# Window attention in float32: scores of two heads per matmul and a product over 128 rows of keys, with zeros where heads or windows differ, and bands fetched at other times

## The chip, the cores and the metric

The kernel runs on one core of one Trainium2 chip. The metric is the device time of one execution in microseconds (us); the kernel before was timed three times, and its time is the median of the three. One further execution was taken with the hardware profiler; its page and trace are what this document reads. TensorE is called PE in the profile (its weight loads PEld), VectorE is DVE, ScalarE ACT, GpSimd POOL and SyncE SP.

## The reference, cut to what matters

The input `x` has 16 images of 56 x 56 pixels with 384 channels, float32.

```python
x = x + attention(groupnorm(x))       # layer 0
x = x + depthwise3x3(groupnorm(x))    # layer 1, weights clipped and taken as signs

def attention(x):                     # shifted windows of 7 x 7
    x = roll(x, (-3, -3), axis=(1, 2))
    q, k, v = split(x @ w_qkv.T, 3)   # 12 heads of 32 channels
    # per image: 64 windows of 49 tokens, 12 heads
    score = q @ k.T / sqrt(32) + relative_position_bias   # 49 x 49 a window and head
    score = where(mask of the last window row / column, -inf, score)
    out = softmax(score) @ v
    return roll(out @ w_out.T + b_out, (3, 3), axis=(1, 2))
```

## The kernel before, in words

**Tiling.** Channels lie on partitions: 384 channels are `NC` = 3 blocks of 128 (four heads of 32 in a block, `HPC`), tokens run along the free dimension. A *strip* `s` is one row of eight windows (8 x 49 = 392 tokens, `ST`); an image has `NS` = 8 strips, the batch 128. A strip is worked in two *units* of four windows (`UW`), so there are 256 units, 16 for each image; below, the first unit of a strip is called even and the second odd.

**One unit** (`heavy` and `all_units`). TensorE's work stands in a list of six slots, written out by hand, and every engine works through its instructions in the program's order. In the even unit the slots are three blocks `value` (v of the next strip, L485) and three blocks `query_key` (q of the next strip, L472); in the odd unit three blocks `query_key` (k of the next strip) and three blocks `project` (L656, this strip's output). Each block is 3 float32 matmuls of 392 columns into one of four rotating PSUM banks; ScalarE copies q, k (L479) and v (L492) out, DVE adds the projected block to `x` (L664). After slot 0 come, for the unit's own windows, `add_up` (L597: a matmul with ones that sums the exponentials over keys), `invert` (L635 logarithm and L636 exponential on ScalarE, then L637 and L638 on DVE), `attend` (L617: attention weights times v; ScalarE copies the result to `ot` at L627) and `divide` (L645 on DVE). The next unit's `scores` (L526) and `softmax` (L543, DVE: scale and bias from PSUM to the tile `es`) come after slot 2 in the even unit (before q is overwritten) and after slot 3 in the odd one; its `exponential` (L561, ScalarE) one slot later. `normalize` (L461) makes the input of the strip after next, in slot 4 of the odd unit.

**Scores and product before.** `scores` makes, per unit, 4 windows x 12 heads = 48 matmuls: 32 channels of one head on the rows, 64 key columns as weights, 49 query columns streamed. Keys come out on partitions: window `w` = 0 of a pair on rows 0 to 48, window 1 on rows 64 to 112, so `es` holds two windows side by side on the partitions. `attend` therefore makes 48 matmuls too: 49 keys of one window on the rows (the lower or the upper half of the array), 32 value channels of one head as weights, 49 columns.

**v by keys.** `turn` (L496, DVE) transposes v in 32 x 32 blocks and `by_key` (L508) moves it with 16 DMAs per strip on SP's queue, in slots 3 and 5 of the even unit, to the tile `vs`, with keys on partitions.

**Light work.** The depthwise layer of the image before, and the loads of the next image, are spread over the units by due times (`at(when, ...)`, in units; a list sorted by time is emptied between slots). `plan_conv` places, for each of six chunks of an image (2 halves x 3 channel blocks, one every `step` = 2.6 units): `band` (L703, SP's queue: 28 rows and their neighbours from DRAM into the one buffer of `bpool`), `pad` (L748, ScalarE, 1624 elements) and `middle` (L778, ScalarE, 1568 elements), both of which read the band, eight `tap` (L784, DVE), `turn_sum` (L791) and eight `store` (L798, SP's queue). `plan_load` places the gathers of the next image's rows: DMAs on POOL's queue (L419), a transpose on DVE (L436) and `arrange` (L448 and L451, ScalarE).

**End.** `plan_last` does the last image's depthwise layer after the last unit, partly on TensorE (`convolve`, L822; `carry`), partly as taps on DVE.

Of the kernel before, what the change touches and what calls it, by code (L numbers as in the profile page):

```python
# [19 lines left out]
NEG = -1.0e30  # L20
# [14 lines left out]
def kernel(  # L35
# [65 lines left out]
    least = const.tile([P, 1], F32, tag="least", name="least")  # L101
    reach = const.tile([P, 2, B * NU], F32, tag="reach", name="reach")
    seen = const.tile([P, B + NC], F32, tag="seen", name="seen")
# [15 lines left out]

    es = const.tile([P, NH, 2, HT], F32, tag="e", name="e")  # L120

# [16 lines left out]
    def clear_more():  # L138
        nc.gpsimd.memset(power, -0.5)
        nc.gpsimd.memset(ones, 1.0)  # L140
        nc.gpsimd.memset(least, LEAST)
        nc.gpsimd.memset(seen, 0.0)
        for t in (qk[:, :, ST:], *hps, *accs):
            nc.gpsimd.memset(t, 0.0)

    def clear_again():
        for t in (qk[:, :, ST:], *spare):
            nc.vector.memset(t, 0.0)
# [41 lines left out]
    def load_bias(queue, first_q, last_q, fast):  # L190


        if not loaded_bias:
            rel = ypool.tile([P, NC, WIN, R], F32, tag="y", name="rel").rearrange("q c h w -> q (c h w)")[:, : T * NH]
            nc.gpsimd.memset(rel, 0.0)
            loaded_bias.append(rel)
        rel = loaded_bias[0]
        flat = rel.rearrange("q (a n) -> q a n", a=WIN)
        for q in range(first_q, last_q):
            qr, qc = divmod(q, WIN)  # L200
            first = qr * REL + qc if fast else (WIN - 1 - qr) * REL + (WIN - 1 - qc)
# [12 lines left out]
        nc.gpsimd.memset(mask, 0.0)  # L214
        for w in range(2):
            queue.dma_start(mask[w * HT : w * HT + T], wmask[0:T, :, 0:T])
        loaded_bias.append(mask)

    def add_bias(fast):
# [5 lines left out]
        for v in range(2):  # L225
            for w in range(2):
                for i in range(HPC):
                    nc.vector.tensor_tensor(
                        bias[:, v, i * NC : (i + 1) * NC, w, :],
                        rel_n[:, i],  # L230
                        mask[:, v].unsqueeze(1).to_broadcast([P, NC, T]),
                        ALU.add,
                    )

# [234 lines left out]
    def query_key(s, m):  # L469
        pq = bank(f"pq_{s}_{m}")  # L470
        for c in range(NC):
# [6 lines left out]
            )  # L478
        nc.scalar.copy(qk[:, m, :ST], pq[:, :ST])  # L479

# [32 lines left out]
    def scores(u, fast):  # L513
# [4 lines left out]
        for j in range(NC):  # L518
            for w in range(2):
                for r in range(2):  # L520
                    for i in range(HPC):
                        part = slice(i * D, (i + 1) * D)
                        q0 = (n * UW + 2 * r + w) * T
                        row, col = (w, r) if fast else (r, w)
                        k0 = (2 * j + col) * T
                        nc.tensor.matmul(  # L526
                            pp[row * HT : (row + 1) * HT, i, k0 : k0 + T],
                            qk[part, NC * fast + j, q0 : q0 + HT],
                            qk[part, NC * (not fast) + j, q0 : q0 + T],
                            start=True,  # L530
                            stop=True,
                        )
        raw[u] = pp

    def softmax(u, fast):

        s = u // UPS
        pp = raw[u]
        e = es.rearrange("k (i j) w q -> k i (j w) q", i=HPC)[:, :, :, :T]
        if fast:  # L540
            flat = es.rearrange("k h w q -> k (h w q)")[:, : NH * 2 * T]
            e = flat.rearrange("k (i n q) -> k i n q", i=HPC, q=T)
        nc.vector.scalar_tensor_tensor(  # L543
            e,
            pp[:, :, : NC * 2 * T].rearrange("q i (n k) -> q i n k", k=T),
            QSCALE,
            bias[:, int(s % NS == NS - 1)].rearrange("q (i j) w k -> q i (j w) k", i=HPC),
            ALU.mult,
            ALU.add,
        )  # L550
        if fast:
# [6 lines left out]
    def exponential(u, fast):  # L558
        if fast:
            flat = es.rearrange("k h w q -> k (h w q)")[:, : NH * 2 * T]  # L560
            nc.scalar.activation(flat, flat, AF.Exp, accum_out=reach[:, 0, u : u + 1])  # L561
            return
# [20 lines left out]

    def by_head(u):

        flat = es.rearrange("k h w q -> k (h w q)")[:, : NH * 2 * T]
        return flat.rearrange("k (h r q) -> k h r q", h=NH, r=2)

    def add_up(u):

        e = by_head(u)
        su = raw[u][:, :, NC * 2 * T : NC * 3 * T]
        for r in range(2):
            for i in range(HPC):
                for w in range(2):
# [3 lines left out]
                        ones[keys, :D],  # L599
                        e[keys, i * NC : (i + 1) * NC, r],  # L600
                        start=True,
# [4 lines left out]
    def attend(u, fast):  # L606
        s, n = divmod(u, UPS)
        if n == 0:
            ots[s] = two.tile([P, NC, ST], F32, tag="ot", name=f"ot_{s}")
        po = [bank(f"po_{u}_{w}") for w in range(2)]  # L610
        for j in range(NC):
            for r in range(2):
                for i in range(HPC):
                    for w in range(2):
                        h = HPC * j + i
                        keys = slice(w * HT, w * HT + T)
                        nc.tensor.matmul(  # L617
                            po[w][i * D : (i + 1) * D, (2 * j + r) * T : (2 * j + r + 1) * T],
                            vs[s][keys, n * 2 + r, h * D : (h + 1) * D],
                            by_head(u)[keys, i * NC + j, r] if fast else pts[u, j][keys, 2 * i + r, :],  # L620
                            start=True,
                            stop=True,
                        )
        ot = ots[s][:, :, n * UW * T : (n + 1) * UW * T]
        by_window = ot.rearrange("p j (r w q) -> p j r w q", r=2, w=2)
        for w in range(2):
            nc.scalar.copy(  # L627
                by_window[:, :, :, w, :], po[w][:, : NC * 2 * T].rearrange("p (j r q) -> p j r q", j=NC, r=2)
            )

# [77 lines left out]
    def band_late(b, k, c, part):  # L708
# [4 lines left out]
        if part == 0:  # L713
# [3 lines left out]
            elif (k, c) == (0, 1):  # L717
                xb = qk.rearrange("p m n -> p (m n)")
            elif (k, c) == (1, 0):
                xb = bias.rearrange("p v h w n -> p (v h w n)")  # L720
            else:
# [82 lines left out]

    def convolve(b, k, c):

# [4 lines left out]
        tiles = LR * W // OT  # L811
        summed[k] = []
        for first in range(0, tiles, 4):
            n = min(4, tiles - first)
            pc = bank(f"pc_{k}_{first}")
            summed[k].append((first, n, pc))
            for i in range(n):
# [13 lines left out]
    def carry(b, k, c):  # L831

        by_token = spare[k].rearrange("p t c -> p (t c)")
        tiles = LR * W // OT
# [30 lines left out]
    def plan_last(b, first):  # L865
# [8 lines left out]
        for n, (k, c) in enumerate(chunks):  # L874
# [27 lines left out]
    def plan_conv(p, first, step, lead, late, queue):  # L902
# [116 lines left out]
    with tc.manual_schedule():  # L1019
# [29 lines left out]
        worst = small.tile([P, 2], F32, tag="worst", name="worst")  # L1049
        for n in range(2):  # L1050
            nc.vector.tensor_scalar(reach[:, n], reach[:, n], MOST[n], None, ALU.is_lt)
        nc.vector.tensor_reduce(worst[:, 0:1], reach.rearrange("p n u -> p (n u)"), AX.X, ALU.min)
# [73 lines left out]
```

## Time and profile before

| | us |
|---|---|
| three timed runs | 4202.64, 4207.44, 4210.01 |
| median | 4207.44 |
| the profiled execution, its whole time | 4213.37 |
| the same, from first to last instruction (span) | 4211.4 |

| engine | busy us | share of the span |
|---|---|---|
| TensorE matmuls | 4068.7 | 97% |
| TensorE weight loads | 2565.1 | 61% |
| DVE | 3495.2 | 83% |
| ScalarE | 2232.3 | 53% |
| POOL | 1863.9 | 44% |

The granted TensorE clock was 0.988 of full speed over the span. How to read the lines: a row of groups has line, engine, operation, output tile <- input tiles, shape, count, then busy time in us and mean ns of one, then the idle time of that engine just before it and what ended most of it. A float32 matmul stands as two records, each with its own weight load. A row of waits has who waited, for whom, total us, how many times, longest. A row of the timeline has start and duration in us, engine, line, operation, and in square brackets the idle time before it with its releaser. Matmul ends are modelled and overlap, so a block of matmuls is best measured from its start to the next block's start.

### The profile page before, as it was taken

The page shows a single profiled execution, that of the slowest core. Times are in us where ns is not written, and L with a number is a line of the kernel's source. Part 1 is how long each engine was busy: PE and PEld are TensorE (multiplying, and loading weights), DVE is VectorE, ACT ScalarE, POOL GpSimd, SP SyncE. Part 2 cuts the span into 40 slices and gives each one's busy share as a digit, 9 for nine tenths or more (in the row PEclk, how much of TensorE's full clock was granted, in tenths as well). Part 3 has the DMA queues.
Part 4 walks back from the last instruction along what each step waited for, and adds up shares of the span by engine and source line. Part 5 has one row for each costly group of instructions (what it writes and reads, how often), then busy time and mean ns, then how long its engine had stood idle before and what let it go on. Part 6 is the DMA issues. An engine that isn't in the chain of part 4 may idle for free.

```text
span 4211.4 us, 153120 instructions
## 1 busy us (share of the span) xinstructions
PE 4068.7 (97%) x67257; PEld 2565.1 (61%) x67257; DVE 3495.2 (83%) x3711; ACT 2232.3 (53%) x4654; POOL 1863.9 (44%) x3165
## 2 busy tenths in 40 slices
PE   5999999999999999999999999999999999999997
PEld 3666566565666666666566666666566566666656
DVE  3556889888898888889888888988989888888897
ACT  2545555555555555555555555655556555554552
POOL 5444435445453554445445453554445445451100
PEclk8999999999999999999999999999999999999998
DMA  4434555654565655556654565655555565554454
GB/s 92 79 63 85 97 107 116 112 111 92 111 122 93 124 109 101 99 106 117 112 115 97 103 121 93 124 112 99 98 112 112 109 121 96 102 119 83 96 109 107
DMA packets 1524021, 439.45 MB, mean 104 GB/s; under 512 B 1458970, under 2 KB 1473979, under 8 KB 1523346
## 3 DMA queue, kind: packets, MB, share of 16 engines
q1 hardware_dynamic: 1432680, 267.66, 37.3%
q0 software_dynamic: 87648, 159.12, 16.2%
q8 instruction: 532, 8.72, 0.9%
q10 hardware_dynamic: 3018, 2.78, 0.3%
q14 instruction: 143, 1.17, 0.1%
HBM read 169.63 MB, written 158.46 MB: 78 GB/s over the span
## 4 chain that ended last, share of the span: by engine, by line
PE 40%; issue 16%; DVE 14%; POOL 12%; DMA 10%; SPq 4%; ACT 3%; DVEq 0%; ACTq 0%; POOLq 0%
PE pq L472 16%; POOL xl L419 9%; PE pv L485 8%; PE py L656 8%; DVE o L784 6%; PE ps L526 3%; SPq L508 3%; PE po L617 3%; DMA xl<-in_x_dram 3%; DMA mid<-y 2%; PE ps L597 2%; DMA xb<-mid 2%; DVE e L543 1%; SPq L798 1%; DVE xt L436 1%
## 5 line engine op out<-in xcount | busy, mean ns | idle before, releaser
L472 PE MATMUL pq<-xn,wq_t 128*128 128x392 f32 x4608 | 1587.0, 497 | 0.3
L419 POOL DMA_DIRECT2D xl<-in_x_dram x1980 | 1332.8, 720 | 172.2 <-DMA mid<-y 59.6
L784 DVE SCALAR_TENSOR_TENSOR o<-hp,dw_t,o 128x1568 f32<-128x1568 f32 x752 | 1378.5, 1833 | 5.4
L472 PEld LDWEIGHTS pq<-xn,wq_t 128*128 128x128 f32 x4608 | 846.3, 188 | 596.6 <-issue 1.6
L485 PE MATMUL pv<-xn,wq_t 128*128 128x392 f32 x2304 | 827.3, 502 | 35.5 <-ACT vt L492 30.6
L656 PE MATMUL py<-ot,wo_t 128*128 128x392 f32 x2304 | 816.2, 499 | 15.1 <-DVE ot L645 15.1
L479 ACT COPY qk<-pq 128x392 f32<-128x392 f32 x768 | 369.2, 483 | 622.4 <-PE pq L472 621.2
L485 PEld LDWEIGHTS pv<-xn,wq_t 128*128 128x128 f32 x2304 | 425.9, 190 | 343.0 <-ACT vt L492 39.4
L676 POOL COPY y<-y 128x63 f32<-128x63 f32 x128 | 46.3, 362 | 1299.0 <-DVE y L664 1299.0
L656 PEld LDWEIGHTS py<-ot,wo_t 128*128 128x128 f32 x2304 | 426.3, 190 | 313.2 <-DVE ot L645 25.6
L637 DVE SCALAR_TENSOR_TENSOR ln<-ps,inv 128x588 f32<-128x588 f32 x256 | 195.3, 763 | 467.7 <-ACT inv L636 467.6
L561 ACT ACTIVATE e<-e 128x1176 f32<-128x1176 f32 x256 | 303.4, 1185 | 456.1 <-DVE e L543 454.2
L492 ACT COPY vt<-pv 128x392 f32<-128x392 f32 x384 | 188.9, 492 | 416.0 <-PE pv L485 415.4
L526 PEld LDWEIGHTS ps<-qk 32*64 32x64 f32 x24576 | 311.3, 132 | 156.5 <-issue 125.2
L617 PE MATMUL po<-e,v 49*32 49x49 f32 x24576 | 374.1, 212 | 12.3 <-DMA v<-vq 10.7
L617 PEld LDWEIGHTS po<-e,v 49*32 49x32 f32 x24576 | 362.6, 105 | 20.5 <-issue 10.2
L543 DVE SCALAR_TENSOR_TENSOR e<-ps,bias 128x1176 f32<-128x1176 f32 x256 | 347.7, 1358 | 17.2 <-PE ps L526 17.0
L526 PE MATMUL ps<-qk 32*64 32x49 f32 x24576 | 345.4, 226 | 9.0 <-issue 6.8
L448 ACT COPY x<-xt 128x196 f32<-128x196 f32 x720 | 225.8, 368 | 175.9 <-DVE xt L436 175.7
L496 DVE STREAM_TRANSPOSE vq<-vt 128x512 f32<-128x512 f32 x384 | 265.9, 694 | 9.6 <-ACT vt L492 6.5
L461 ACT ACTIVATE xn<-x,coef 128x392 f32<-128x392 f32 x384 | 247.1, 712 | 14.4 <-DMA coef<-cod 14.4
L664 DVE TENSOR_TENSOR y<-py,x 128x392 f32<-128x392 f32 x384 | 213.4, 556 | 44.7 <-PE py L656 44.1
(173 smaller groups left out, 3351.4 us busy)
## 6 DMA issues: line engine op xcount, KB each, us to landing
v<-vq SPq DMA_DIRECT2D x2048, 48.0 KB
xb<-mid SPq DMA_DIRECT2D x90, 855.5 KB
out_dram<-o SPq DMA_DIRECT2D x736, 98.0 KB
mid<-y POOLq DMA_DIRECT2D x112, 619.5 KB
xl<-in_x_dram POOLq DMA_DIRECT2D x1260, 52.5 KB
mid<-y POOLq DMA_DIRECT2D x15, 354.0 KB
xl<-in_x_dram POOLq DMA_DIRECT2D x180, 28.0 KB
mid<-y POOLq DMA_DIRECT2D x15, 265.5 KB
```

What stands on the lines that cost most here:

```text
L419: nc.gpsimd.dma_start(xz[i * D + lo : i * D + hi, c, k : k + n, :], flat[token : token + n * (hi - lo)].rearrange("(k t) c -> t k c", k=n) ...
L461: nc.scalar.activation(xn[:, c, :, :T], xs[s][:, c, :].rearrange("p (w t) -> p w t", t=T), AF.Identity, bias=coef[:, c, 1:2], scale=coef[: ...
L472: nc.tensor.matmul(pq[:, :ST].rearrange("p (w t) -> p w t", t=T), wq_t[:, c, m * P : (m + 1) * P], xn[:, c, :, :T], start=(c == 0), stop=( ...
L479: nc.scalar.copy(qk[:, m, :ST], pq[:, :ST])
L485: nc.tensor.matmul(pv[:, :ST].rearrange("p (w t) -> p w t", t=T), wq_t[:, c, 2 * C + m * P : 2 * C + (m + 1) * P], xn[:, c, :, :T], start= ...
L496: nc.vector.transpose(vq[:, :, :, m].rearrange("p h n d -> p n h d"), vt[:, m].rearrange("p (n w) (j b) -> p n (w j) b", w=2, b=D),)
L526: nc.tensor.matmul(pp[row * HT : (row + 1) * HT, i, k0 : k0 + T], qk[part, NC * fast + j, q0 : q0 + HT], qk[part, NC * (not fast) + j, q0 ...
L543: nc.vector.scalar_tensor_tensor(e, pp[:, :, : NC * 2 * T].rearrange("q i (n k) -> q i n k", k=T), QSCALE, bias[:, int(s % NS == NS - 1)]. ...
L561: nc.scalar.activation(flat, flat, AF.Exp, accum_out=reach[:, 0, u : u + 1])
L617: nc.tensor.matmul(po[w][i * D : (i + 1) * D, (2 * j + r) * T : (2 * j + r + 1) * T], vs[s][keys, n * 2 + r, h * D : (h + 1) * D], by_head ...
L656: nc.tensor.matmul(py[:, :ST], wo_t[:, c, m * P : (m + 1) * P], ots[s][:, c, :], start=(c == 0), stop=(c == NC - 1),)
L784: nc.vector.scalar_tensor_tensor(acc, by_half(hp[:, dy : dy + BR, dx : dx + W]), dw_t[:, c, t : t + 1], acc, ALU.mult, ALU.add)
```

## The change

- The query tile `qk` is split into `kt` (keys) and `qd` (queries). Each query block is written twice by ScalarE, with a per-partition factor `mine` that is 1 for even heads in the first copy (`a` = 0), 1 for odd heads in the second and 0 elsewhere.
- `scores` then takes two heads (64 rows) at once: the weights are 64 key columns of both heads, the streamed operand 2 x 49 query columns, first head then second; what would mix the heads is zero. 24 matmuls of 98 columns instead of 48 of 49.
- The tile `es` becomes `eb` with room for two windows behind each other on the free dimension. `softmax` writes the scores of both windows (lower and upper partitions) to the place `w` = 0; `exponential` runs twice, with a per-partition bias `own` of -1e30 on the partitions of the other window: first into `w` = 1, then in place into `w` = 0. So each place holds one window's weights and zeros on the other window's partitions.
- `attend` then takes all 128 rows of keys at once: 24 matmuls of 98 columns (two windows) instead of 48 of 49.
- `bias` is kept once for both windows (half the size, 8 additions instead of 16), padding rows are masked with -1e30, and tiles that the last image's depthwise layer borrowed are exchanged (`qd`, `eb`, `bias` for `qk`, `bias`, `es`).
- `band` is placed at `max(when - 1.22 * step, first - lead + 0.5)` instead of `when - 0.75 * step`. In the end part, `convolve` is split in two and `turn_late` comes 0.15 later.

The rest of the diff concerns the second, careful version of the kernel that runs only where values overflow.

```diff
-    bias = const.tile([P, 2, NH, 2, T], F32, tag="bias", name="bias")
+    bias = const.tile([P, 2, NH, T], F32, tag="bias", name="bias")
...
-    qk = const.tile([P, 2 * NC, ST + HT - T], F32, tag="qk", name="qk")
+    kt = const.tile([P, NC, ST + HT - T], F32, tag="k", name="kt")
+    qd = const.tile([P, NC * 2 * ST + HT - T], F32, tag="q", name="qd")
+    queries = qd[:, : NC * 2 * ST].rearrange("p (m w a q) -> p m w a q", m=NC, a=2, q=T)
+    mine = const.tile([P, 2], F32, tag="mine", name="mine")
...
-    es = const.tile([P, NH, 2, HT], F32, tag="e", name="e")
+    eb = const.tile([P, NH * 2 * 2 * T], F32, tag="e", name="e")
...
+        for w in range(2):
+            nc.gpsimd.memset(own[w * HT : (w + 1) * HT, w : w + 1], 0.0)
+            nc.gpsimd.memset(own[w * HT : (w + 1) * HT, 1 - w : 2 - w], NEG)
...
+        for i in range(HPC):
+            for a in range(2):
+                nc.gpsimd.memset(mine[i * D : (i + 1) * D, a : a + 1], float(i % 2 == a))
...
-        nc.scalar.copy(qk[:, m, :ST], pq[:, :ST])
+        if m >= NC:
+            nc.scalar.copy(kt[:, m - NC, :ST], pq[:, :ST])
+            return
+        for a in range(2):
+            nc.scalar.activation(
+                queries[:, m, :, a],
+                pq[:, :ST].rearrange("p (w q) -> p w q", q=T),
+                AF.Identity,
+                scale=mine[:, a : a + 1],
+            )
...
+                            part = slice(i * HT, (i + 1) * HT)
+                            nc.tensor.matmul(
+                                pp[w * HT : (w + 1) * HT, 2 * r + i, 2 * j * T : 2 * (j + 1) * T],
+                                kt[part, j, at * T : at * T + HT],
+                                queries[part, j, at].rearrange("p a q -> p (a q)"),
+                                start=True,
+                                stop=True,
+                            )
...
         if fast:
+            nc.vector.scalar_tensor_tensor(
+                eb.rearrange("k (r p n w q) -> k r p n w q", r=2, p=2, w=2, q=T)[:, :, :, :, 0],
+                pp[:, :, : NC * 2 * T].rearrange("k (r p) (n q) -> k r p n q", r=2, q=T),
+                QSCALE,
+                added.rearrange("k (p n) q -> k p n q", p=2).unsqueeze(1).to_broadcast([P, 2, 2, 2 * NC, T]),
+                ALU.mult,
+                ALU.add,
+            )
...
-            flat = es.rearrange("k h w q -> k (h w q)")[:, : NH * 2 * T]
-            nc.scalar.activation(flat, flat, AF.Exp, accum_out=reach[:, 0, u : u + 1])
+            e = eb.rearrange("k (n w q) -> k n w q", w=2, q=T)
+            for w in (1, 0):
+                nc.scalar.activation(
+                    e[:, :, w],
+                    e[:, :, 0],
+                    AF.Exp,
+                    bias=own[:, w : w + 1],
+                    accum_out=reach[:, 2 * w, u : u + 1],
+                )
...
+                    here = po[r][i * D : (i + 1) * D, 2 * j * T : 2 * (j + 1) * T]
+                    if fast:
                         nc.tensor.matmul(
+                            here,
+                            vs[s][:, n * 2 + r, value],
+                            by_head()[:, r, i // 2, j, i % 2].rearrange("k w q -> k (w q)"),
                             start=True,
                             stop=True,
                         )
...
-                    at(when + 1.15 + 0.01 * half, turn_late, b, k, c, half, n == len(chunks) - 1)
+                    at(when + 1.3 + 0.01 * half, turn_late, b, k, c, half, n == len(chunks) - 1)
...
-            at(when + 0.1, convolve, b, k, c)
+            at(when + 0.1, convolve, b, k, c, 0)
+            at(when + 0.4, convolve, b, k, c, 1)
...
-            at(when - 0.75 * step, band, p, k, c)
+            at(max(when - 1.22 * step, first - lead + 0.5), band, p, k, c)
```

More of the change, by code (lines that the diff above doesn't have):

```diff
@@ L101 @@
     least = const.tile([P, 1], F32, tag="least", name="least")
-    reach = const.tile([P, 2, B * NU], F32, tag="reach", name="reach")
+    reach = const.tile([P, 3, B * NU], F32, tag="reach", name="reach")
     seen = const.tile([P, B + NC], F32, tag="seen", name="seen")
@@ L118 @@
     xt = const.tile([P, NC, NR, D], F32, tag="xt", name="xt")
-    es = const.tile([P, NH, 2, HT], F32, tag="e", name="e")
+    eb = const.tile([P, NH * 2 * 2 * T], F32, tag="e", name="e")
+    es = eb[:, : NH * 2 * HT].rearrange("p (h w k) -> p h w k", w=2, k=HT)
+    own = const.tile([P, 2], F32, tag="own", name="own")
     hps = [const.tile([P, BR + 2, W + 2], F32, tag=f"hp{n}", name=f"hp{n}") for n in range(2)]
@@ L225, in add_bias @@
         for v in range(2):
[L226 to L233, printed above, removed]
+            for i in range(HPC):
+                by_row = bias[:, v].rearrange("q (i j) k -> q i j k", i=HPC)[:, i]
+                if fast:
+                    by_row = bias[:, v].rearrange("q (p j a) k -> q p j a k", j=NC, a=2)[:, i // 2, :, i % 2]
+                nc.vector.tensor_tensor(
+                    by_row,
+                    rel_n[:, i],
+                    mask[:, v].unsqueeze(1).to_broadcast([P, NC, T]),
+                    ALU.add,
+                )
     stats, coefs, parts = {}, {}, {}
@@ L538, in softmax @@
         pp = raw[u]
-        e = es.rearrange("k (i j) w q -> k i (j w) q", i=HPC)[:, :, :, :T]
+        added = bias[:, int(s % NS == NS - 1)]
         if fast:
-            flat = es.rearrange("k h w q -> k (h w q)")[:, : NH * 2 * T]
[L542 to L551, printed above, removed]
-            return
+            nc.vector.scalar_tensor_tensor(
[4 more added lines that the diff above has]
+                ALU.mult,
+                ALU.add,
+            )
+            return
+        for i in range(HPC):
+            of_i = slice(i * NC, (i + 1) * NC)
+            for w in range(2):
+                nc.vector.scalar_tensor_tensor(
+                    es[:, of_i, w, :T],
+                    pp[:, i, : NC * 2 * T].rearrange("q (j w k) -> q j w k", w=2, k=T)[:, :, w],
+                    QSCALE,
+                    added[:, of_i],
+                    ALU.mult,
+                    ALU.add,
+                )
         e = es.rearrange("q h w k -> q (h w) k")[:, :, :T]
@@ L609, in attend @@
             ots[s] = two.tile([P, NC, ST], F32, tag="ot", name=f"ot_{s}")
-        po = [bank(f"po_{u}_{w}") for w in range(2)]
+        po = [bank(f"po_{u}_{r}") for r in range(2)]
         for j in range(NC):
@@ L623, in attend @@
                         )
[L624 to L629, printed above, removed]
+                        continue
+                    for w in range(2):
+                        keys = slice(w * HT, w * HT + T)
+                        nc.tensor.matmul(
+                            here[:, w * T : (w + 1) * T],
+                            vs[s][keys, n * 2 + r, value],
+                            pts[u, j][keys, 2 * i + r, :],
+                            start=True,
+                            stop=True,
+                        )
+        ot = ots[s][:, :, n * UW * T : (n + 1) * UW * T].rearrange("p j (r q) -> p j r q", r=2)
+        for r in range(2):
+            nc.scalar.copy(ot[:, :, r], po[r][:, : NC * 2 * T].rearrange("p (j q) -> p j q", j=NC))
     def invert(u):
@@ L717, in band_late @@
             elif (k, c) == (0, 1):
-                xb = qk.rearrange("p m n -> p (m n)")
+                xb = qd
             elif (k, c) == (1, 0):
-                xb = bias.rearrange("p v h w n -> p (v h w n)")
+                xb = eb
             else:
@@ L811, in convolve @@
         tiles = LR * W // OT
-        summed[k] = []
-        for first in range(0, tiles, 4):
+        for first in (4 * part,):
             n = min(4, tiles - first)
             pc = bank(f"pc_{k}_{first}")
-            summed[k].append((first, n, pc))
+            summed.setdefault(k, []).append((first, n, pc))
             for i in range(n):
@@ L831, in carry @@
     def carry(b, k, c):
-        by_token = spare[k].rearrange("p t c -> p (t c)")
+        by_token = spare[k].rearrange("p t c -> p (t c)") if k else bias.rearrange("p v h k -> p (v h k)")
         tiles = LR * W // OT
@@ L1049 @@
         worst = small.tile([P, 2], F32, tag="worst", name="worst")
-        for n in range(2):
-            nc.vector.tensor_scalar(reach[:, n], reach[:, n], MOST[n], None, ALU.is_lt)
+        for n in range(3):
+            nc.vector.tensor_scalar(reach[:, n], reach[:, n], MOST[n % 2], None, ALU.is_lt)
         nc.vector.tensor_reduce(worst[:, 0:1], reach.rearrange("p n u -> p (n u)"), AX.X, ALU.min)
```

47 lines of the change are left out of this document (22 added, 25 removed).

## The prediction

> **What bounds the kernel now.** I read the page first, then the waits, then the timeline of one strip (two units of four windows), engine by engine.
>
> ```profile
> PE 4068.7 (97%) x67257; PEld 2565.1 (61%) x67257; DVE 3495.2 (83%) x3711; ACT 2232.3 (53%) x4654; POOL 1863.9 (44%) x3165
> ...
> L472 PE MATMUL pq<-xn,wq_t 128*128 128x392 f32 x4608 | 1587.0, 497 | 0.3
> ...
> L561 ACT ACTIVATE e<-e 128x1176 f32<-128x1176 f32 x256 | 303.4, 1185 | 456.1 <-DVE e L543 454.2
> ...
> L617 PE MATMUL po<-e,v 49*32 49x49 f32 x24576 | 374.1, 212 | 12.3 <-DMA v<-vq 10.7 <-ACT qk L479 0.6
> ...
> L526 PE MATMUL ps<-qk 32*64 32x49 f32 x24576 | 345.4, 226 | 9.0 <-issue 6.8
> ```
>
> TensorE is in use nearly all the time. Every float32 product stands as two records (24576 for 48 x 256), and scores and product together hold 720 us of it. DVE, at 83%, is the next engine.
>
> ```profile
> 2081.62 0.73 PE L597 MATMUL ps<-e,ones 49*32 49x147 f32 x32
> 2082.15 1.63 PE L617 MATMUL po<-e,v 49*32 49x49 f32 x96
> 2083.71 4.22 PE L485 MATMUL pv<-xn,wq_t 128*128 128x392 f32 x12
> 2087.85 1.32 PE L526 MATMUL ps<-qk 32*64 32x49 f32 x96
> 2089.10 8.17 PE L472 MATMUL pq<-xn,wq_t 128*128 128x392 f32 x24
> 2097.20 0.74 PE L597 MATMUL ps<-e,ones 49*32 49x147 f32 x32
> 2097.73 1.27 PE L617 MATMUL po<-e,v 49*32 49x49 f32 x96
> 2098.93 4.22 PE L472 MATMUL pq<-xn,wq_t 128*128 128x392 f32 x12
> 2102.99 2.13 PE L656 MATMUL py<-ot,wo_t 128*128 128x392 f32 x6
> ```
>
> Columns are start, duration, engine, line. A block costs its start to the next block's start: scores 1.25 us, product 1.20 in the odd unit and 1.56 in the even one, sums 0.53. The difference between the products is that in even units the first matmuls each wait for two DMA queues of v; the line has 996 separate wait instructions, 7.8 per strip.
>
> ```profile
> 2091.38 0.49 ACT L479 COPY qk<-pq 128x392 f32<-128x392 f32 x1 [2.93 <-PE pq L472]
> 2091.76 1.19 ACT L561 ACTIVATE e<-e 128x1176 f32<-128x1176 f32 x1
> ...
> 2093.36 0.49 ACT L479 COPY qk<-pq 128x392 f32<-128x392 f32 x1 [0.32 <-PE pq L472]
> 2095.33 0.49 ACT L479 COPY qk<-pq 128x392 f32<-128x392 f32 x1 [1.49 <-PE pq L472]
> 2097.30 0.49 ACT L479 COPY qk<-pq 128x392 f32<-128x392 f32 x1 [1.49 <-PE pq L472]
> 2098.04 0.75 ACT L635 ACTIVATE ln<-ps,least 128x588 f32<-128x588 f32 x1 [0.25 <-PE ps L597]
> ...
> 2101.32 0.77 DVE L645 TENSOR_TENSOR ot<-ot,ln 128x588 f32<-128x588 f32 x1
> ```
>
> This is ScalarE between the first of the three query copies and the logarithm of the odd unit. Its idle time (in brackets) after the exponential is 0.32 + 1.49 + 1.49 + 0.25 = 3.55 us. What follows the logarithm is a tight chain: L636, then L637, L638 and L645 on DVE, whose end at 2102.09 releases `project` at 2102.99. **Only 0.9 us stand between ScalarE's lateness and TensorE there.**
>
> ```profile
> ACT hp L748 <- DMA xb<-mid: 104.0, 16, 8.6
> ...
> PEld py L656 <- DVE ot L645: 25.6, 25, 3.2
> ...
> PE pv L485 <- ACT vt L492: 30.6, 14, 2.7
> ```
>
> Once per image `pad` waits for its band (some 7 us, 16 times); the value copy stands behind it in ScalarE's order and TensorE waits in turn.
>
> **Scores (gain).** 48 matmuls of 49 columns become 24 of 98 on 64x64 tiles, of which four fit. A record of 392 columns takes 4.06/12 = 0.338 us, so one of 98 takes 0.084; 48 records, four abreast, are 12 rounds, 1.01 us. Leaving a tiled block for a full one costs some 0.09 (a value block of 12 records before the scores takes 4.14, a query block before `project` 4.06). That is 1.10; I take 1.12 with the filling. 256 x (1.25 - 1.12) = **-33 us**, bounds -10 and -55 (the block's mean is 1.33, as some are held up).
>
> **Product (gain).** 24 matmuls of 98 columns on 128x32 tiles, again four abreast: 1.01 + 0.09, and 0.09 more since the sums before it use 64-row tiles and now the shape changes. That is 1.20, nothing in odd units. In even units the order of the changed program shows four first matmuls with two waits where eight had them; two of those waits are hidden under the sums already, so I take 1.30 for 1.56: 128 x 0.26 = **-33 us**, bounds 0 and -55.
>
> A row speaks for four abreast: the 32 records of the sums, 147 columns each, take 0.53 us, against 32 x 0.127 = 4.1 one by one, so nearly eight ran at a time on only two halves of rows, four column groups in each. The Trainium skill, "TensorE: Matmul & The Clock Gate", Part 3, says the contrary for this change: a weight load overlaps matmuls in flight only where the row group differs, and a 128-row tile takes all of them. Its 27 ns for 32 columns would then lie in series with every record, 48 x (84 + 27) ns = 5.3 us a block, an estimate from that page, and the whole would be some 1000 us slower. The row of the sums disagrees, so I do not use it.
>
> **Bands (gain).** The late one is the fourth of six. By the plan's own times (3 + 3 x 2.6 = 10.8, less 0.75 and 0.35 of 2.6) it is issued 8.85 units after the image's start and wanted at 9.89, and on SP's queue it stands behind eight v copies. The change puts it at 7.63, right behind `middle` of the band before it, whose buffer it needs. SP then waits for that ScalarE instruction with v copies and stores queued behind; v is wanted over a unit later, so I cost that at nothing (up to 1 us x 90 bands if not). The blocks after the wait (value, 45 us over their usual length in all, and the query blocks some 18 us later, 12 us) come back: **-57 us**, bounds -40 and -59.
>
> **ScalarE (cost).** The exponential doubles: 1.18 from start to start becomes two of about 1.27 (a bias operand more), +1.36 us a unit. Three query copies a strip become two ACTIVATEs each with a scale operand. Their price lies between the copy's 0.483 (same source, no operand) and L461's 0.712 (same elements, two operands); I take 0.59, 0.49 from start to start, so +0.60 each. Between first query copy and logarithm that is 1.36 + 3 x 0.60 = 3.15 us. In the strip above 3.55 idle us swallow it. In others the gather of the next images' rows (some 0.8 us a time), `pad` (1.76) or `middle` (1.71) lie there: at 1931 to 1939 us nothing is idle after the exponential and the logarithm comes 2.55 late. Done strip by strip with the idle times of the timeline, the eight strips from 1850 to 2110 us come out 0.8, 1.8, 2.5, 0.9, 0.8, 2.5, 1.1 and 0 late, less slacks at `project` of 0.85, 0.74, 0.06, 0.77, 0.47, 0 (the logarithm itself has 1.1 there, as DVE is late), 0.77 and 0.77: waits of 5.7 us. Over all 128 strips it is 78 us; where the band's wait goes, some 7 of it go too. **+71 us**, bounds 30 and 115.
>
> **Exponential to sums (cost).** The sums wait for the longer exponential. In even units its end lies 1.1 to 1.2 us ahead of the sums in a quarter of the units, elsewhere 2.4 and more; 1.36 more leaves short waits: **+15 us**, bounds 5 and 30.
>
> **Small edits.** DVE's L543 keeps its 1176 elements (0 to +0.2 us, inside the slack just named). Twelve memsets at the start, some 0.26 us each, lie on POOL before an 11 us wait: nothing, 3 us if uncovered. The last unit's exponential is on the path; a fourth PSUM bank is held longer by query copies; in the tail, DVE's taps stand back to back and set the time, so split convolution and later turn are worth nothing: together **+5 us**, bounds -5 and +10.
>
> **Sum.** -33 - 33 - 57 + 71 + 15 + 5 = -32 us. The profiled execution took 4213.4 (span 4211.4), the median 4207.4, so I carry the difference over: 4175. I give **4178**, as some of the gain in even units meets the same v transfers.
>
> **Rivals.** *ScalarE keeps up* (chance 0.25): the waits at `project` do not come, for instance because each query copy is nearer to L479's price and the gathers fall elsewhere. For it: it has 47% idle. Against it: the 0.9 us slack. Without +71 and half of the +15: about 4100.
>
> *ScalarE sets the pace of the odd unit* (0.22), slower: query copies at L461's price (0.61 start to start, +0.24 x 3 a strip) and DVE, blocked longer at L637, late again at L543. The gains are 123 us less 20, 0.80 us a strip; mean waits at `project` over 0.80 us decide it, my reading is 0.56. At 115 to 150 us of waits: 4220 to 4255. Against it: the PSUM row of a copy is cheaper than the SBUF row.
>
> *Tiles do not run four abreast* (0.05): at two abreast each block is 2.1 us, +0.85 x 512, some 4600.
>
> *The band still comes late* (0.05), because SP is held at its new place: +57, 4235.
>
> **How the numbers follow.** The forecast itself has 0.43, its own range 4130 to 4225. Differences under 0.2% (8.4 us) a measurement of this kernel can't tell from none. Of the forecast 0.28 lies below 4199, 0.08 within, 0.07 above; with the first rival 0.25 faster, and 0.02 of the second within: faster 0.53, same 0.10, slower 0.37. The range 4090 to 4270 leaves out the slow tiles, the low end of the first rival and the far end of the second, under 0.2.
>
> **What would show it.** Half as many records on the scores' and product's lines; blocks of 1.12 and 1.20; scores and product in the even unit without the long start; no wait of `pad` for xb; ScalarE busy near 2850; PEld or PE `py` waiting for L645 by some 70 us more than now. Wrong if the blocks do not shrink (tiles), if `py` waits under 30 us (first rival) or over 120 (second), or if pv still waits for vt 14 times.

## The result and the profile after

The changed kernel takes 4258.44 us (median of four runs, 4256.83 to 4260.11); the kernel before stands at 4206.39 (four runs). The ratio is 1.0123, with a 95% interval from 1.0110 to 1.0136: slower by 52 us. The forecast was 4178; the time lies inside its range, on the other side of no change. The profiled execution of the kernel after took 4256.83 us (span 4255.0), 43 more than that of before.

First the rows of the page that answer to those shown of before:

```profile
PE 4033.8 (95%) x42681; PEld 2416.5 (57%) x42681; DVE 3493.3 (82%) x3704; ACT 2796.1 (66%) x5550; POOL 1827.6 (43%) x3178
...
L488 PE MATMUL pq<-xn,wq_t 128*128 128x392 f32 x4608 | 1586.4, 497 | 34.9 <-ACT qd L499 34.8
...
L605 ACT ACTIVATE e<-e,own 128x1176 f32<-128x1176 f32 x512 | 664.5, 1298 | 525.1 <-DVE e L576 515.8
L713 PE MATMUL py<-ot,wo_t 128*128 128x392 f32 x2304 | 824.5, 503 | 53.7 <-DVE ot L702 52.3
...
L499 ACT ACTIVATE qd<-pq,mine 128x392 f32<-128x392 f32 x768 | 403.2, 582 | 240.2 <-PE pq L488 239.2
...
L667 PE MATMUL po<-e,v 128*32 128x98 f32 x12288 | 321.2, 251 | 7.5 <-DMA v<-vq 6.6
...
L551 PE MATMUL ps<-qd,kt 64*64 64x98 f32 x12288 | 317.8, 248 | 1.6 <-DVE ln L694 1.6
```

The records of scores and product are halved, as announced, and their busy time fell from 720 to 639 us. ScalarE is busy 564 us more, where the prediction's prices gave 579 (256 x 1.36 + 384 x 0.60). TensorE has less to do and is idle more: the query blocks, which before stood at 0.3 us of idle time, now have 34.9, and `project` 53.7, the first behind ScalarE's query copies, the second behind DVE's L702, which stands behind ScalarE's logarithm. The waits of TensorE (who waits, for whom, total, times, longest) show a third place, the sums:

```profile
PE ps L646 <- ACT e L605: 62.6, 60, 8.2
PE py L713 <- DVE ot L702: 52.3, 55, 2.1
PE pq L488 <- ACT qd L499: 34.8, 45, 1.5
```

The next lines are the timeline of one odd unit after, its ScalarE, and the PE and DVE lines that depend on it.

```profile
2050.07 1.30 ACT L605 ACTIVATE e<-e,own 128x1176 f32<-128x1176 f32 x1 [1.48 <-DVE e L576]
...
2051.27 0.18 ACT L605 ACTIVATION_READ_ACCUMULATOR e<-e,own 128x1 f32 x1
2051.49 1.30 ACT L605 ACTIVATE e<-e,own 128x1176 f32<-128x1176 f32 x1
2052.69 0.19 ACT L605 ACTIVATION_READ_ACCUMULATOR e<-e,own 128x1 f32 x1
2052.79 1.04 ACT L499 ACTIVATE qd<-pq,mine 128x392 f32<-128x392 f32 x2
...
2053.33 0.73 PE L646 MATMUL ps<-e,ones 49*32 49x147 f32 x32
2053.73 0.61 ACT L464 COPY x<-xt 128x196 f32<-128x196 f32 x2
...
2054.49 1.07 ACT L499 ACTIVATE qd<-pq,mine 128x392 f32<-128x392 f32 x2
...
2055.44 0.48 ACT L496 COPY kt<-pq 128x392 f32<-128x392 f32 x1
...
2055.61 4.22 PE L488 MATMUL pq<-xn,wq_t 128*128 128x392 f32 x12 [0.40 <-ACT qd L499]
2055.81 0.77 ACT L692 ACTIVATE ln<-ps,least 128x588 f32<-128x588 f32 x1
...
2059.22 0.77 DVE L702 TENSOR_TENSOR ot<-ot,ln 128x588 f32<-128x588 f32 x1
...
2060.04 2.24 PE L713 MATMUL py<-ot,wo_t 128*128 128x392 f32 x6 [0.21 <-DVE ot L702]
```

From the first exponential to the key copy ScalarE has no gap. The second exponential starts 1.42 us after the first, because the reading of the running sum stands between them, and the pair takes 2.72 us from start to end (1.18 before); I had taken 2.54. The last query copies end at 2055.56, and the key block (`query_key`, L488) that needs the PSUM bank they read starts at 2055.61: the wait that I had not priced. The logarithm starts 2.5 us after the sums (0.84 before), and `project` follows L702 by 0.05 us.

The table adds up, over the whole run, the time from the start of one block of TensorE to the start of the next, for the kernel before, the band's line alone, the kernel with one exponential and one query copy ("one of each", an experiment below) and the kernel after. Each number includes the waits in front of the next block.

| block, us in the run | before | bands alone | one of each | after |
|---|---|---|---|---|
| value to sums (even) and query to sums (odd) | 1299 | 1299 | 1299 | 1356 |
| sums to product | 139 | 139 | 178 | 176 |
| product, even unit | 216 | 208 | 158 | 154 |
| product, odd unit | 153 | 154 | 146 | 187 |
| blocks ahead of the scores | 836 | 791 | 792 | 799 |
| scores | 331 | 321 | 298 | 298 |
| query to `project` | 529 | 515 | 520 | 580 |
| `project` to value | 511 | 511 | 511 | 511 |
| sum | 4013 | 3937 | 3902 | 4061 |

Outside these blocks, at the start and the end, the run has 199 us before and 194 after, and DVE's softmax takes 1357 ns where it took 1358. The kernel with one of each has the smaller parts of the change too, so they do not make the loss.

### The profile page after: what moved, and what is told of

It is laid out like the page before. It is cut to its first block, busy times and chain, and to the rows that moved or that the text cites. A ratio compares the mean times of both kernels' runs of the same rounds, so it can differ in the third digit from the quotient of the medians.

```text
span 4255.0 us, 104793 instructions
## 1 busy us (share of the span) xinstructions
PE 4033.8 (95%) x42681; PEld 2416.5 (57%) x42681; DVE 3493.3 (82%) x3704; ACT 2796.1 (66%) x5550; POOL 1827.6 (43%) x3178
## 4 chain that ended last, share of the span: by engine, by line
issue 30%; POOL 19%; PE 18%; DVE 17%; DMA 8%; ACT 7%; SPq 0%; DVEq 0%; ACTq 0%; POOLq 0%
POOL xl L435 12%; DVE o L841 7%; PE pq L488 6%; PE py L713 4%; PE pv L510 4%; ACT e L605 3%; DMA mvd<-mv 2%; DVE e L576 2%; DMA xl<-in_x_dram 2%; DMA gt<-mvd 1%; ACT qd L499 1%; POOL dev L284 1%; PE ps L551 1%; PE po L667 1%; POOL mid L737 1%
## 5 line engine op out<-in xcount | busy, mean ns | idle before, releaser
L488 PE MATMUL pq<-xn,wq_t 128*128 128x392 f32 x4608 | 1586.4, 497 | 34.9 <-ACT qd L499 34.8
L488 PEld LDWEIGHTS pq<-xn,wq_t 128*128 128x128 f32 x4608 | 845.2, 188 | 653.5 <-ACT qd L499 44.7
L605 ACT ACTIVATE e<-e,own 128x1176 f32<-128x1176 f32 x512 | 664.5, 1298 | 525.1 <-DVE e L576 515.8
L713 PE MATMUL py<-ot,wo_t 128*128 128x392 f32 x2304 | 824.5, 503 | 53.7 <-DVE ot L702 52.3
L510 PE MATMUL pv<-xn,wq_t 128*128 128x392 f32 x2304 | 813.6, 496 | 1.7 <-ACT xn L477 1.2
L733 POOL COPY y<-y 128x63 f32<-128x63 f32 x128 | 36.8, 287 | 1458.3 <-DVE y L721 1458.1
L499 ACT ACTIVATE qd<-pq,mine 128x392 f32<-128x392 f32 x768 | 403.2, 582 | 240.2 <-PE pq L488 239.2
L576 DVE SCALAR_TENSOR_TENSOR e<-ps,bias 128x1176 f32<-128x1176 f32 x256 | 347.4, 1357 | 13.0 <-PE ps L551 13.0
L468 DVE BATCH_NORM_STATS2 st<-x 128x6 f32<-128x392 f32 x360 | 200.1, 559 | 184.3 <-ACT x L467 184.3
L551 PEld LDWEIGHTS ps<-qd,kt 64*64 64x64 f32 x12288 | 268.7, 133 | 144.2 <-issue 106.7
L667 PE MATMUL po<-e,v 128*32 128x98 f32 x12288 | 321.2, 251 | 7.5 <-DMA v<-vq 6.6
L551 PE MATMUL ps<-qd,kt 64*64 64x98 f32 x12288 | 317.8, 248 | 1.6 <-DVE ln L694 1.6
L667 PEld LDWEIGHTS po<-e,v 128*32 128x32 f32 x12288 | 261.0, 110 | 70.7 <-issue 66.1
L496 ACT COPY kt<-pq 128x392 f32<-128x392 f32 x384 | 185.3, 484 | 122.6 <-PE pq L488 121.6
```

Source lines behind the costliest of these rows:

```text
L488: nc.tensor.matmul(pq[:, :ST].rearrange("p (w t) -> p w t", t=T), wq_t[:, c, m * P : (m + 1) * P], xn[:, c, :, :T], start=(c == 0), stop=( ...
L499: nc.scalar.activation(queries[:, m, :, a], pq[:, :ST].rearrange("p (w q) -> p w q", q=T), AF.Identity, scale=mine[:, a : a + 1],)
L510: nc.tensor.matmul(pv[:, :ST].rearrange("p (w t) -> p w t", t=T), wq_t[:, c, 2 * C + m * P : 2 * C + (m + 1) * P], xn[:, c, :, :T], start= ...
L551: nc.tensor.matmul(pp[w * HT : (w + 1) * HT, 2 * r + i, 2 * j * T : 2 * (j + 1) * T], kt[part, j, at * T : at * T + HT], queries[part, j, ...
L576: nc.vector.scalar_tensor_tensor(eb.rearrange("k (r p n w q) -> k r p n w q", r=2, p=2, w=2, q=T)[:, :, :, :, 0], pp[:, :, : NC * 2 * T].r ...
L605: nc.scalar.activation(e[:, :, w], e[:, :, 0], AF.Exp, bias=own[:, w : w + 1], accum_out=reach[:, 2 * w, u : u + 1],)
```

## The experiments

My theory was that TensorE's gains and the bands' are real, and that the doubled work of ScalarE takes back more than both; the rivals blamed TensorE's new tile shapes, or the bands' new place on SP's queue. All times are medians, and each ratio is to the kernel before as it was timed beside that run (4205 to 4212 us).

**The band's line alone**, on the kernel before:

```diff
-            at(when - 0.75 * step, band, p, k, c)
+            at(max(when - 1.22 * step, first - lead + 0.5), band, p, k, c)
```

> The kernel before with only the band fetch moved to its new place. My theory (the bands are a gain of their own; all of the loss comes from ScalarE's extra work): pad no longer waits for xb, the value blocks lose their 45 us of waits and the query blocks before project 12 us, so about 4150 us, 55 us below the kernel before. Rival (the earlier place on SP's queue holds up the copies of v and the stores behind it, and this is part of the loss): 4190 us or more, with new waits for v or for the bands.

Measured: 4134.91 us against 4211.43, ratio 0.9815 (0.9795 to 0.9835). The bands give 77 us, more than the 40 to 59 forecast. By the table 44 of them lie in the blocks ahead of the scores, 11 in the scores, 8 in the even products and 14 at `project`: `pad`, late, had pushed ScalarE's later work as well. The wait of `project` for L645 shows it, first in the kernel before, then in this one:

```profile
PE py L656 <- DVE ot L645: 15.1, 12, 3.0
```

```profile
PE py L656 <- DVE ot L645: 3.0, 1, 3.0
```

This kernel is faster than the kernel before and the kernel after.

**The same the other way round**: the kernel after with the bands' old due times (the line above undone).

> The changed kernel with the band fetch at its old place. My theory: the waits of pad come back, some 3 us of TensorE in each of 15 images and 12 us behind them: 4300 to 4315 us, 45 to 57 us above the changed kernel. Rival (in the changed kernel ScalarE is late anyway and hides the transfer, so the earlier bands brought nothing there): within 10 us of the changed kernel.

Measured: 4318.38 us, ratio 1.0255 (1.0232 to 1.0279). That is a little above the 4300 to 4315 expected, and the line is worth 60 us in the changed kernel (58 by the blocks of the table). The waits of TensorE in this run show the one that it removes, beside the new ones, which stay:

```profile
PE ps L646 <- ACT e L605: 77.2, 70, 8.2
PE py L713 <- DVE ot L702: 52.8, 56, 2.1
PE pq L488 <- ACT qd L499: 39.4, 47, 1.5
PE pv L510 <- ACT vt L517: 24.3, 14, 2.2
```

**The scores alone, with the bands**: the kernel after with a single exponential in place, and the 48 small matmuls of the product as before.

```diff
-            for w in (1, 0):
...
+            e = eb.rearrange("k (n w q) -> k n w q", w=2, q=T)[:, :, 0]
+            nc.scalar.activation(e, e, AF.Exp, accum_out=reach[:, 0, u : u + 1])
```

> Scores of two heads per matmul with the doubled query copies and the earlier bands; the exponential is done once and the product is made of 48 matmuls, as before. My theory: scores blocks 1.17 us as in the changed kernel (33 us gained against the bands alone), ScalarE 3 x 0.6 us a strip later, which mostly fits into its idle time, so 20 to 40 us of waits come back at project: 4120 to 4160 us, about level with the bands alone. Rival (TensorE's change of tile shapes and not ScalarE makes the loss): the same place within 10 us of the bands alone minus 33, that is about 4117, and the loss sits in the product alone.

Measured: 4136.84 us, ratio 0.9819 (0.9799 to 0.9840), no better than the bands alone. Its blocks of the scores fall to 298 us, 23 less than with the bands alone; but its stretch from query to `project` is 545 us instead of 515. The query copies, which the scores need twice, cost there what the wider matmuls give. The page has it in one row:

```profile
L698 PE MATMUL py<-ot,wo_t 128*128 128x392 f32 x2304 | 819.5, 501 | 27.5 <-DVE ot L687 26.4
```

**The product alone, with the bands**: scores of one head as before, two exponentials and 128 rows of keys (the change's own lines, without those on the queries and the scores).

> The product over 128 rows with the doubled exponential and the earlier bands; scores of one head each and one copy of the queries, as before. My theory: 40 us less in the product blocks of even units and 10 us more in odd ones, against 57 us of waits of the sums for the exponential and 30 to 40 us at project: 4190 to 4220 us, 40 to 70 us above the bands alone. Rival (the waits come from the query copies that stand before the exponential in ScalarE's order): no more than 20 us above the bands alone.

Measured: 4200.49 us, ratio 0.9973 (0.9963 to 0.9983): 66 us worse than the bands alone. Sums and product together have 14 us less, the blocks ahead of the sums 33 more, `project` 39 more.

**ScalarE's doubled parts, one at a time**, in the kernel after: the exponential for window 0's place only (first edit: "one exponential"), the query copy for the even heads only (second: "one query copy"), and both edits ("one of each"). Half of the attention weights, or the scores of half the heads, are left out; the places that nobody writes are filled once at the start.

```diff
-            for w in (1, 0):
+            for w in (0,):
...
-        for a in range(2):
+        for a in range(1):
```

> The changed kernel without the second exponential: the place of window 1 keeps a constant, so half of the attention weights are not computed; TensorE's and DVE's work is the same. My theory: the waits of the sums for the exponential (57 us) go, and those at project and for PSUM banks shrink by more than half (60 of 104 us): 4130 to 4160 us. Rival (the loss lies in TensorE's blocks and their change of shape): 4240 us or more.

> The changed kernel without the second copy of the queries (the odd heads' queries stay zero, so their scores are not computed); the exponential is doubled. My theory: the query blocks no longer wait for PSUM banks (41 us) and project waits less (20 to 30 of 63 us), the waits of the sums stay: 4180 to 4210 us. Rival (the doubled exponential alone carries the loss, query copies fit into idle time): within 15 us of the changed kernel.

> The changed kernel with neither the second exponential nor the second query copy (left out as in the two runs beside it); TensorE has all of the change's shapes. My theory: all of the ScalarE waits go, and what is left is the gain on TensorE and of the bands: 4075 to 4105 us. Rival (TensorE's shapes cost as much as they bring): at the bands alone, about 4150 us, or above.

Measured: one exponential 4133.51 (ratio 0.9832, 0.9813 to 0.9850), one query copy 4191.93 (0.9970, 0.9960 to 0.9980), one of each 4099.82 (0.9749, 0.9731 to 0.9767). In the last one TensorE does all the matmuls of the kernel after and hardly waits:

```profile
PE 4011.5 (98%) x42681; PEld 2428.7 (59%) x42681; DVE 3494.9 (85%) x3705; ACT 2291.9 (56%) x4654; POOL 1868.9 (46%) x3179
...
L490 PE MATMUL pq<-xn,wq_t 128*128 128x392 f32 x4608 | 1587.7, 497 | 0.1
...
L715 PE MATMUL py<-ot,wo_t 128*128 128x392 f32 x2304 | 816.8, 500 | 4.5 <-DVE ot L704 4.4
```

So TensorE's shapes do not make the loss. From here, the second query copies alone cost 34 us, the second exponential alone 92, both together 159: 33 more than their sum. The wait on a PSUM bank behind the query copies comes nearly only with both: the odd products of the table take 146 us with one exponential, 146 with one of each, 152 with one query copy and 187 after. The waits of the kernel with one query copy:

```profile
PE ps L646 <- ACT e L605: 46.8, 60, 8.2
PE py L713 <- DVE ot L702: 40.1, 33, 2.1
...
PE pq L488 <- ACT qd L499: 4.8, 13, 0.5
```

With one exponential the sums do not wait more than with one of each (1299 us in the table's first row), and `project` takes 553.

**No running sums in the exponentials**:

```diff
                     bias=own[:, w : w + 1],
-                    accum_out=reach[:, 2 * w, u : u + 1],
```

> The kernel after, with both exponentials but without their running sums (the record of the largest values of the exponential is left out and stays zero). My theory: the two exponentials take 2.72 us from start to end, where I had priced 2.54, because the reading of the sum (0.19 us) stands between the two; without it they take some 2.5 us, the waits at sums, banks and project fall in the proportion that one exponential showed (92 to 125 us for 1.54 us), so 15 to 25 us less than the kernel after: 4233 to 4246 us. The rival: what costs is the second pass over 1176 elements alone, and the reading lies beside it; then 4253 to 4262 us.

Measured: 4235.94 us against 4212.33, ratio 1.0055 (1.0038 to 1.0072), 22 us less than the kernel after (the blocks of the table fall by 22 as well). The time is as expected, and the readings do stand in the way, both of them. From start to end the pair fell from 2.72 to 2.63 us, as its line shows. The second reading holds back what comes after the pair: where nothing else waits, the next instruction starts 1.20 us after the second exponential, in the kernel after 1.30 (medians of 189 units each). So from the first exponential to the next instruction it is 2.54 us instead of 2.72, near the 2.5 expected. Of the 256 x 0.18 = 46 us of ScalarE about half came back as time, where I had reckoned with a quarter to a third.

```profile
2057.21 2.63 ACT L606 ACTIVATE e<-e,own 128x1176 f32<-128x1176 f32 x2 [3.86 <-DVE e L577]
```

**Old tiles, with the product ahead of the sums** in even units, on the kernel with the bands alone:

```diff
+                    early = fast and u % UPS == 0
+                    if early:
+                        attend(u, fast)
                     if fast:
                         add_up(u)
...
-                    attend(u, fast)
+                    if not early:
+                        attend(u, fast)
```

> The bands' line alone on the kernel before (4135 us), and in even units the product of 48-row tiles now ahead of the sums, so that its eight first matmuls, each with two waits for the queues of v, stand behind a value block of 12 long records instead of behind the short records of the sums. My theory: most of the gain in the even unit's product (1.62 to 1.15 us a block) came from the number of those waits, not from the 128-row tiles; behind long records they are hidden, the even product falls to some 1.2 us, 128 x 0.4 = 50 us, and the logarithm of the even unit, 1.2 us later, has slack there. So 4080 to 4105 us. The rival: the 128-row tiles themselves, or the arrival of v, made the gain; then the block stays near 1.6 and the time is 4125 to 4145.

Measured: 4144.14 us against 4212.33, ratio 0.9835 (0.9819 to 0.9852): a miss, 9 us above the bands alone. The time is where the rival had put it, but the product did not stay near 1.6 us. The timeline of this kernel shows both halves of the answer: a strip where it worked, 1.60 us from the product to the next value block, and the next strip with 2.46.

```profile
2074.99 1.05 PE L617 MATMUL po<-e,v 49*32 49x49 f32 x93
...
2075.91 0.75 PE L597 MATMUL ps<-e,ones 49*32 49x147 f32 x29
2076.59 4.22 PE L485 MATMUL pv<-xn,wq_t 128*128 128x392 f32 x12
...
2105.38 1.36 PE L617 MATMUL po<-e,v 49*32 49x49 f32 x93
...
2106.59 0.75 PE L597 MATMUL ps<-e,ones 49*32 49x147 f32 x29
2107.84 4.22 PE L485 MATMUL pv<-xn,wq_t 128*128 128x392 f32 x12 [0.50 <-DVE y L664]
```

SP's line for the second strip:

```profile
2098.61 5.51 SPq L508 DMA_DIRECT2D v<-vq  x8
```

The median of sums and product together in even units is 1.60 us, against 2.10 with the sums first and 1.82 in the kernel after. So the waits that stand alone can be hidden with the old tiles too, in about half of these units (66 of 127 take less than 1.75 us). But a quarter of them take 2.35 us or more, the run's sum over these blocks falls by 11 us only, and the value and `project` blocks take that back. In the second strip 0.50 of the 0.86 us too many is a wait of the value block for DVE's L664, as its line says; and the last v copies leave SP's queue at 2104.12, 1.3 us ahead of a product that now comes half a microsecond sooner. Both waits have grown over the run. With the bands alone they were:

```profile
PE po L617 <- DMA v<-vq: 10.2, 10, 5.7
...
PE pv L485 <- DVE y L664: 3.1, 12, 0.4
```

With the product first:

```profile
PE po L617 <- DMA v<-vq: 18.0, 26, 5.4
...
PE pv L485 <- DVE y L664: 6.5, 11, 0.9
```

Which of them makes the slow units was not isolated.

## Why the prediction was wrong

The gains were forecast at 123 us and came to 111 (before to "one of each" in the table, 4013 to 3902); the costs were forecast at 91 us and came to 159. The forecast was lost on the costs, and there in two terms.

**Exponential to sums: +15 forecast, +57 measured** (1356 against 1299). This is the step that failed first. I took the pair at +1.36 us where it is +1.54, and I read the slack ahead of the sums as before, as if everything else on ScalarE and DVE stayed in place. It did not: in even units the median time from the exponential's end to the sums fell from 2.48 to 0.41 us, 0.5 more than the longer pair explains, and L576 itself starts later after the scores (median 2.76 us, before 2.11). The lost slack weighs more than the size of the pair: an estimate from the slacks of the run with the bands alone, each even unit by itself, gives 14 us of waits for a pair longer by 1.36 and 21 for 1.54, and none in odd units; measured were 48 in even and 9 in odd units. What took the slack is known in part: with one query copy the first row still has 42 of the 57 us, so most of it comes with the second exponential alone.

**PSUM banks: nothing forecast, +41 measured.** The prediction named the bank held longer by the query copies and put it into +5 us of small edits. Each strip's query copies were priced only for the logarithm behind them; that TensorE waits for the same copies, one block earlier, was not worked out.

**`project`: +71 forecast, +60 measured** (580 against 520). The strip-by-strip reading of ScalarE's gaps came near in the sum, less so in the strips: the eight strips that the prediction went through wait 0.2, 1.0, 1.9, 0.3, 0.9, 0.4, 0 and 0 us in the kernel after, where it had 0, 1.1, 2.4, 0.1, 0.3, 1.4, 0.3 and 0. Its 5.7 us make 91 over 16 images; how they became 78 it does not show. A query copy takes 582 ns, and I had taken 590. Another 8 us stand before the scores that follow the first `project` block.

**Scores: -33 forecast, -23 measured** (321 to 298). The block's median fell from 1.25 to 1.17 us, not to 1.12. Against the kernel before the row falls by 33, but 11 of these come with the band's line. The 0.09 us that the prediction adds for leaving a tiled block was read from a value block ahead of the scores, so from the way into them; that block takes 4.15 us after as before, and no row shows the price of the way out.

**Product: -33 forecast, -18 measured**, by other parts than I gave. In odd units 1.20 fell to 1.15, where I had forecast nothing, and in even units 1.57 to 1.15, where I had forecast 1.30: together -58. But the change of shape between sums and product lengthens the sums' block from 0.53 to 0.66 us, 0.13 where I had taken 0.09, and that row of the table rises by 40 (256 x 0.13 = 33, the rest in single units). The Trainium skill, "TensorEngine Tiling (Array Packing)", Key Properties, says that a change of tiling mode drains TensorE. The sums' block agrees, with 0.13 us from their tiles of 64 rows to the product's of 128; the change from a query block to the sums shows no price, as two query blocks ahead of the sums take 8.10 us, no more than twice the 4.06 of one ahead of `project`.

**Tiles four abreast: right.** The rule of the Trainium skill, "TensorE: Matmul & The Clock Gate", Part 3, by which weight loads of 128-row tiles could not overlap, would have given 5.3 us a block as an estimate. The measured block is 1.15 us, and the measurement decides.

**Bands: -57 forecast, -77 measured alone, -60 in the changed kernel.** In the changed kernel it is at the upper bound (59). Alone it is above it, as the earlier band there also takes waits from ScalarE's later work.

**The rivals.** "ScalarE sets the pace" had the right sign and nearly the time (4220 to 4255), and DVE is late at the softmax, as it said (L576, 2.76 against 2.11 us). But its query copies at L461's price and its more than 0.80 us of waits at `project` did not come: a query copy takes 582 ns and L461's counterpart 711, and those waits are 0.47 us a strip. "ScalarE keeps up" is refuted; its 4100 us is the time of the kernel that spares ScalarE the doubled work (4099.82). Slow tiles are refuted by the blocks of 1.15 and 1.17 us, and a late band by ScalarE, which no longer waits for xb. ScalarE busy "near 2850" was no sum of the prediction's own prices (2232 + 579 = 2811); 2796 was measured.

Where the two additions to ScalarE cost 33 us more together than apart, the rows of the table tell: 35 more in the bank waits and 15 more ahead of the sums, 14 less at `project`. Versions that take other work off ScalarE, such as the copies of the gathered rows, were not tried.

## What to carry to other kernels

Filling an operand with zeros makes fewer and wider matmuls, but some engine has to write the operand twice; here that was 564 us of work on an engine that was at 53%, for some 41 us on TensorE. When an engine beside the critical path gets more work, list every place where the critical engine meets it (the operand, the bank it must free, the result at the end) and lay the whole strip out anew, since the slacks of the trace of before may be gone in the trace of after. Try each part of a combined change alone: no kernel here that does all of the work is faster than the one with the bands' line alone, 1.85% faster than before.

## What the runs showed of the hardware

Half as many records, each twice as wide, saved only 0.05 us (product, odd units) to 0.08 us (scores) of a block of some 1.2 us. The change from the sums' tiles of 64 rows to the product's of 128 cost 0.13 us in each unit. The reading of an accumulated sum takes 0.19 us on ScalarE, but only 0.09 of it keeps the next instruction waiting. A bias taken from a column of a tile made the exponential 1298 ns; without one it took 1206 in the kernel of the scores alone, at the same places of the tile, and 1185 in the kernel before. A query copy from PSUM with a scale from a column took 582 ns, a plain copy of as many elements 484; it also writes its elements to other places, and the two were not separated.
